# Other shares and other queues for side work: shift sums, helper taps and weight forms in a fused transformer and ConvNeXt kernel

## The chip, the cores and the metric

The kernel runs on one core of a Trainium2 chip. The metric is the device time of one execution in microseconds (us), as the median of several runs. Five engines work in parallel, each on its own instructions in their order: TensorE (PE, matrix products), VectorE (DVE), ScalarE (ACT), GpSimd (POOL) and SyncE (SP). POOL and SP are used here to issue DMAs.

## The reference

For eight images of 384 channels and 32 x 32 pixels, in float32, two layers are computed:

```python
# layer 0, on N = 1024 tokens of C = 384 channels
xn  = layernorm(xf, g1, beta1)
q, k, v = split(einsum('bnc,oc->bno', xn, w_qkv) + b_qkv)        # 8 heads of 48
out = softmax(q @ k.T * 48 ** -0.5) @ v
x1  = einsum('bnc,oc->bno', out, w_proj) + b_proj + xf
h   = gelu(einsum('bnc,oc->bno', layernorm(x1, g2, beta2), w_fc1) + b_fc1)   # 1536 wide
y   = x1 + einsum('bnh,oh->bno', h, w_fc2) + b_fc2
# layer 1, on the image of y
z = depthwise_conv_7x7(y, dw_w) + dw_b
z = gelu((layernorm(z) * ln_w + ln_b) @ w1 + b1)
nx = l2norm_over_pixels(z) / (mean_over_channels(...) + 1e-6)
z = grn_gamma * (z * nx) + grn_beta + z
return y + (z @ w2 + b2)
```

Shifts that the layers add before a product (ln_b, grn_beta, beta1, beta2) are folded into the bias after it: the kernel computes the sums `ln_b @ w1` and `grn_beta @ w2` itself, once, and calls them shift sums here.

## The kernel before

Tokens lie along the free axis and channels on the 128 partitions: an image is a tile of 3 x 1024 columns (`CT` = 3 channel tiles). The images run one after the other. Of image b, PE does the products for q, k and v, then attention (32 steps for each half of the tokens: scores, exponential on ACT, product with v), the projection and the MLP. The second layer's products of image b-1 follow in the same round. The depthwise convolution has no product: DVE does it tap by tap into `acc` (L1102, 42 of 49 taps), during the next image's attention and MLP.

*The helper.* The remaining taps, `HELPED` = 7 of each channel tile and two more in image 0, go another way (`help_convolution`): ACT multiplies half an image by the tap's weight into a tile "res" (L1123), and POOL issues a DMA that adds it to `acc` (L1124). "res" has four buffers. `norm_of_next`, which normalises the next image early, draws its places from the same four (L1717 issues its folds, DMAs that add one half of the partitions to the other). A list `quiet` holds the helper back: while it is not empty, `help_convolution` yields in steps of 1 us, and 3 us more afterwards.

*The order.* All instructions are written out in one order by `Flow`. Each piece of side work is a generator which yields a number of us; `flow.pe(us)` is called behind every piece of PE work and steps the generators that have come due in that planned time. `flow.finish(chain)` writes all that is left of one at once. `end_soon` and `end_convolution` finish the helper and the convolution before the second layer's norm, which the code does in the MLP of each image from 1 on. Each engine then takes its own instructions strictly in this order.

*PSUM.* Pool `ps_s` has two buffers of [128, 1024] (scores, tag "s"), `ps_o` four of [128, 512] (tag "o"). `gelu_half` makes one hidden tile of the MLP in an o buffer, and ACT applies gelu to it (`hid`, L457). In the last image, `mlp_by_halves` does the MLP in two halves of the tokens.

*Image 0.* Beside its attention and MLP the kernel prepares weights: `shift_through_w1` and `shift_through_w2` make the shift sums (DVE scales and adds, a matmul with ones sums the columns into an s buffer, and DVE adds the bias to that, L1501 and L1519, tile `b_f`). `sums_singly` (L1376) and `forms` make sums of weight blocks for a matrix product scheme with fewer multiplications and store them in DRAM (`s_w1`, `s_w2`); `forms` loads its parts as `w_a` and `w_b` and stores them as `s_w`. The MLP's own transfers on POOL are `fc_e<-hid` (L887), `hid<-hid` (L969) and the folds of a norm's sums (`token_sums`, L478), which the matmuls `ln_sum` and `ln_var` (L484) read.

Of the kernel before, what the change touches and what calls it, by code (L numbers as in the profile page):

```python
# [46 lines left out]
F32 = mybir.dt.float32  # L47
AF = mybir.ActivationFunctionType
# [127 lines left out]
def block_kernel(  # L176
# [84 lines left out]
    def o_tile(name):  # L261
        return ps_o.tile([P, NH], F32, tag="o", name=name)

    def weighted(dst, part, name, k):

        if k == 0:
            nc.vector.tensor_scalar(dst, part, col(name, 0), None, ALU.mult)
        else:
            nc.vector.scalar_tensor_tensor(dst, part, col(name, k), dst, ALU.mult, ALU.add)
# [102 lines left out]
            flow.pe(2 * U)  # L372
        return ps

    def linear_half(lhsT, rhs, nk, h, name):
        ps = o_tile(name)
        for k in range(nk):
            nc.tensor.matmul(out=ps, lhsT=lhsT(k), rhs=rhs(k)[:, half(h)], start=(k == 0), stop=(k == nk - 1))  # L378
            flow.pe(U)
        return ps  # L380
# [76 lines left out]
        nc.scalar.activation(dst, src, function, **kw)  # L457
        table[0] = None

    def s_tile(name):  # L460
        return ps_s.tile([P, N], F32, tag="s", name=name)

    def token_sums(t, name, fold, wait, bank):

        width = t.shape[-1]
        if fold is None:
            total = o_tile(name)[:, :width]
            nc.tensor.matmul(out=total, lhsT=ones, rhs=t, start=True, stop=True)  # L470
            flow.pe(U * width / NH)
            return [(total, slice(0, width))]
        rows = [slice(0, 64), slice(64, P)]
        parts = [(fold, slice(0, width))]
        if fold == "columns":
            parts = [(j, slice(j * width // 2, (j + 1) * width // 2)) for j in range(2)]
        for j, cols in parts:
            nc.gpsimd.dma_start(out=t[rows[j], cols], in_=t[rows[1 - j], cols], accum_op=ALU.add)  # L478
        yield wait
        totals = []  # L480
        for j, cols in parts:
            total = bank(f"{name}_{j}")[:, : cols.stop - cols.start]
            for i in rows:
                nc.tensor.matmul(out=total[i, :], lhsT=ones[rows[j], :64], rhs=t[rows[j], cols], start=True, stop=True)  # L484
            flow.pe(U * width / NH / 2)
            totals.append((total, cols))
        return totals

    def layernorm(src, dst, h, eps, g, name, switch, spare=None, spaced=False, slow=1.0, fold=None, wait=3.4, gentle=False, bank=o_tile, late=0):

# [14 lines left out]
            yield 1.2  # L505
        nc.vector.tensor_tensor(a, a, src[:, 2, cols], ALU.add)
        yield 2.6 * slow
        totals = yield from token_sums(a, f"{name}_sum{h}", fold, wait, bank)
        yield 0.8
        for ct in range(CT):  # L510
            for total, part in totals:
# [14 lines left out]
            yield 1.2  # L526
        nc.vector.tensor_tensor(squares[0], squares[0], squares[2], ALU.add)
        yield 1.8 * slow
        totals = yield from token_sums(squares[0], f"{name}_var{h}", fold, wait, bank)
        yield 0.8  # L530

        if not spare:
# [59 lines left out]
    def qk(b, xn, weights=None):  # L592
# [64 lines left out]
        if weights:  # L657
            for _ in fast(0):
                pass
            rest_of_k = fast(1)  # L660
            for n in rest_of_k:
                if n == 9:
                    break
            return parts[:, 0], parts[:, 1], last_tile, ready
# [82 lines left out]
    def attention(b, xt, qT, kT, last_tile, ready, first, next_image):  # L747
# [44 lines left out]
        for n in range(len(steps) + 2):  # L792
            if n == 2:
                last_tile()
            if n < len(steps):
                if steps[n][0] == 0 and steps[n][2] == 0:
                    ready(steps[n][1])
                ps[n] = scores(*steps[n])
            if n >= 2:
                product(*steps[n - 2], ps.pop(n - 2))  # L800
            if n - 2 in (len(steps) // 2 - 9, len(steps) - 9):
                quiet.append("averages")
            if n - 2 == len(steps) // 2 + 6:
                for chain in first:
                    flow.finish(chain)
                xn = one.tile([P, CT, N], F32, tag="xn", bufs=2, name=f"xn2_{b}")
                next_image(b)
                for m in (NP - 1, *range(CT)):
                    flow.finish(chains[0, m])
                proj(b, xt, 0)  # L810
                quiet.clear()
                slow = 1.2 if b in (1, B - 1) else 1.0
                fold = "columns" if b else None
                ln = layernorm(xt, xn, 0, eps0, "g2", f"ln2_{b}", False, spaced=True, slow=slow, fold=fold, wait=4.5)
                ln = flow.spawn(ln)
# [57 lines left out]
                    nc.sync.dma_start(out=other, in_=own)  # L873
                proj("x", xt, qt * P // NH)

    def gelu_half(hid, m, h, xn, weights, wname, name):
        w = weights.at(wname, m // CM)[:, m % CM * CT : (m % CM + 1) * CT, :]
        ps = linear_half(lambda k: w[:, k, :], lambda k: xn[:, k, :], CT, h, f"{name}_{h}_{m}")
        other_table(hid[:, m, half(h)], ps, AF.Gelu, bias=bfc1[:, m : m + 1])

    def difference(dst, more, less):
# [150 lines left out]
    def mlp_by_halves(b, xt, xn, weights, ln, rest, between):  # L1032

        hid = one.tile([P, HT * N], F32, tag="big", name=f"hid_{b}").rearrange("p (m n) -> p m n", m=HT)
        for h in range(2):
            wa, wb = f"fc1_{b}_{h}", f"fc2_{b}_{h}"
            flow.finish(ln)
            for m in range(HT):
                gelu_half(hid, m, h, xn, weights, wa, f"fc1_{b}")
                if m % CM == CM - 1:  # L1040
                    weights.used(wa, m // CM)
                if m == 5 and h == 0:
# [61 lines left out]
            n += 1  # L1104
            yield share * next((early for m, early in first if n <= m), us)

    def help_convolution(acc, us, taken, helped):

        yield 8.0
        for ct in reversed(range(CT)):  # L1110
            taken[ct] = float("inf")
            for i in TAPS[KS * KS - helped :]:
                dy, dx = divmod(i, KS)
                for h in range(2):
                    if quiet:
# [210 lines left out]
    def folds(weights):  # L1326
# [34 lines left out]
                )  # L1361
        nc.vector.tensor_tensor(bout, ps[:, :CT], columns("bproj"), ALU.add)

    def sums_singly(w, store, spare):


# [25 lines left out]
        yield 0.6  # L1392
        plus(r[7], r[14], a22, ALU.subtract)
        plus(r[4], a21, a22)
        yield 0.6
        plus(r[2], a33, r[4], ALU.subtract)
        plus(r[4], r[4], a31)
        yield 0.6
        plus(r[1], a32, r[4])
        minus(r[9], a21, a12)  # L1400
        yield 0.6
        plus(r[9], r[9], a31, ALU.subtract)
        plus(r[0], a31, r[6], ALU.subtract)
        yield 0.6
        nc.vector.tensor_scalar(r[12], a12, -1.0, None, ALU.mult)
        nc.vector.tensor_scalar(r[14], r[14], -1.0, None, ALU.mult)
        yield 1.0
# [2 lines left out]
    def prepare(weights, aside):  # L1410
# [72 lines left out]
        def shift_through_w1():  # L1483
            for i in range(0, HT // 2, CT):
# [12 lines left out]
                for r, a in enumerate((0, 5)):  # L1497
                    for k in range(CT):
                        column_sums(ps, r * CT + k, t[:, k, a, :])
                    m = i + r * HT // 2  # L1500
                    nc.vector.tensor_tensor(b1[:, m : m + CT], ps[:, r * CT : (r + 1) * CT], columns("b1")[:, m : m + CT], ALU.add)  # L1501

        def shift_through_w2():
            for r in range(CT):
# [3 lines left out]
                yield 14.0  # L1508
                h = HT // 2
                for s in range(2):  # L1510
                    g = columns("gbeta")[:, s * h : (s + 1) * h].unsqueeze(2).to_broadcast((P, h, P))
                    nc.vector.tensor_tensor(t[:, s], t[:, s], g, ALU.mult)
                nc.vector.tensor_tensor(t[:, 0], t[:, 0], t[:, 1], ALU.add)
                for k in range(1, h):
                    nc.vector.tensor_tensor(t[:, 0, 0, :], t[:, 0, 0, :], t[:, 0, k, :], ALU.add)
# [3 lines left out]
                nc.vector.tensor_tensor(b2[:, r : r + 1], ps[:, :1], col("b2", r), ALU.add)  # L1519

        if aside:
            yield from shift_through_w1()
# [92 lines left out]
    def main():  # L1615
# [172 lines left out]
        def last_convolution(h, ct, ln=None):  # L1788
# [224 lines left out]
```

## Time and profile before

| | us |
|---|---|
| runs, lowest to highest | 3268.78 to 3273.15 |
| median of three runs | 3271.25 |
| profiled execution, device time | 3271.23 |
| its span in the trace | 3269.3 |
| PE busy | 3231.1 |
| DVE busy | 2423.7 |
| ACT busy | 1670.5 |
| POOL busy | 487.1 |
| mean granted PE clock | 0.995 |

The profile shows one execution. A line of its timeline has the start in us, the time to the end of the group, engine, line of the kernel, operation, written and read tiles, shapes, the number of instructions, and in brackets the idle time before it with what ended that. Its waits list, for a line of an engine, the total of such idle time, how often and the longest. A matmul of 512 float32 columns takes 0.43 us here from start to start where the clock is at 1.00.

### The profile page before, as it was taken

How to read it: one execution, taken by the hardware profiler on the slowest of the kernel's cores; microseconds unless marked ns; L12 is line 12 of the kernel's file. 1: busy time of each engine (PE TensorE's matmuls, PEld its weight loads, DVE VectorE, ACT ScalarE, POOL GpSimd, SP SyncE). 2: the span in 40 equal slices, each digit the busy share in tenths (PEclk: the TensorE clock that was granted, in tenths of full speed). 3: DMA queues.
4: the chain of work that ended last, by engine and by line, in shares of the span. 5: the costliest groups of instructions: out<-in, count | busy, mean ns of one | idle time of the engine just before them, and what ended most of it. 6: DMA issues, size and time to landing. Idle time of an engine off the chain costs nothing. (4 is left out here: it accounts for less than half of the span.)

```text
span 3269.3 us, 38881 instructions
## 1 busy us (share of the span) xinstructions
PE 3231.1 (99%) x14204; PEld 1396.2 (43%) x14204; DVE 2423.7 (74%) x3309; ACT 1670.5 (51%) x2328; POOL 487.1 (15%) x575
## 2 busy tenths in 40 slices
PE   9999998999999999999999999999999999999999
PEld 5334433344344433444344443344434444344455
DVE  4644786678877878678787787876878778879940
ACT  3452664365743566434754537636475365723641
POOL 2111212102211121101212012110121102200000
PEclk9999998999999999999999999999999999999999
DMA  6535744638426473355734465353843638433231
GB/s 214 213 106 121 165 89 75 140 100 193 95 60 161 110 172 80 66 158 125 153 75 98 131 166 125 62 127 105 198 94 58 149 100 196 79 79 91 63 97 54
DMA packets 204114, 387.70 MB, mean 119 GB/s; under 512 B 41232, under 2 KB 46992, under 8 KB 203536
## 3 DMA queue, kind: packets, MB, share of 16 engines
q0 software_dynamic: 82880, 169.38, 27.5%
q1 hardware_dynamic: 120752, 215.09, 21.7%
q8 instruction: 114, 1.87, 0.2%
q10 hardware_dynamic: 288, 0.71, 0.1%
q14 instruction: 80, 0.66, 0.1%
HBM read 199.61 MB, written 38.14 MB: 73 GB/s over the span
## 5 line engine op out<-in xcount | busy, mean ns | idle before, releaser
L1102 DVE SCALAR_TENSOR_TENSOR acc<-pad,vec,acc 128x930 f32<-128x930 f32 (+8 forms) x855 | 956.9, 1156 | 29.2 <-DMA acc<-tap 24.4
L767 ACT ACTIVATE p<-s 128x1024 f32<-128x1024 f32 x512 | 524.3, 1025 | 273.2 <-PE s L758 266.4
L758 PE MATMUL s<-qk 48*64 48x512 f32 x4096 | 539.9, 594 | 5.8 <-DVE b_f L1519 5.6
L778 PE MATMUL o<-p,v 64*64 64x512 f32 x4096 | 536.4, 591 | 0.0
L378 PE MATMUL fc<-xn,fc 128*128 128x512 f32 x1152 | 507.6, 597 | 17.4 <-ACT hid L457 15.3
L1124 POOL DMA_DIRECT2D acc<-tap x306 | 263.4, 874 | 1449.1 <-ACT tap L1123 727.7
L378 PEld LDWEIGHTS fc<-xn,fc 128*128 128x128 f32 x1152 | 218.0, 191 | 302.8 <-issue 271.6
L445 PE MATMUL fc_p<-hid,fc 128*128 128x512 f32 x728 | 318.1, 593 | 2.6 <-DMA hid<-hid 2.0
L778 PEld LDWEIGHTS o<-p,v 64*64 64x64 f32 x4096 | 163.8, 133 | 278.7 <-issue 270.8
L758 PEld LDWEIGHTS s<-qk 48*64 48x64 f32 x4096 | 159.4, 133 | 285.8 <-issue 221.4
L457 ACT ACTIVATE hid<-fc,bfc_f 128x512 f32<-128x512 f32 x192 | 129.4, 684 | 288.1 <-PE fc L378 287.9
L445 PE MATMUL o_p<-y,w 128*128 128x512 f32 x624 | 270.9, 592 | 0.0
L1123 ACT ACTIVATE tap<-pad,vec 128x512 f32<-128x512 f32 x306 | 224.6, 734 | 19.6 <-DMA acc<-tap 19.6
L445 PEld LDWEIGHTS fc_p<-hid,fc 128*128 128x128 f32 x728 | 137.6, 190 | 179.8 <-issue 170.1
L445 PEld LDWEIGHTS o_p<-y,w 128*128 128x128 f32 x624 | 118.0, 190 | 148.7 <-issue 134.9
L1102 DVE SCALAR_TENSOR_TENSOR acc_last<-pad,vec,acc_last 128x377 f32<-128x377 f32 (+24 forms) x288 | 177.2, 690 | 0.6
L891 ACT COPY pad<-x 128x512 f32<-128x512 f32 x48 | 30.2, 635 | 256.2 <-DVE x L957 197.9
L719 DVE TENSOR_TENSOR attn<-o,attn 128x512 f32<-128x512 f32 x64 | 44.1, 690 | 128.9 <-ACT attn L717 128.9
L700 PE MATMUL proj<-attn,wproj_sb 128*128 128x512 f32 x288 | 127.3, 595 | 0.2 <-DVE attn L745 0.2
L678 PE MATMUL v<-wv_sb,xn 128*128 128x384 f32 x384 | 126.8, 487 | 0.0
L432 DVE TENSOR_TENSOR y<-h_n,y 128x512 f32<-128x512 f32 x72 | 49.8, 692 | 62.2 <-PE h_n L416 59.8
L678 PEld LDWEIGHTS v<-wv_sb,xn 128*128 128x128 f32 x384 | 72.5, 190 | 50.1 <-issue 3.3
(376 smaller groups left out, 4052.6 us busy)
## 6 DMA issues: line engine op xcount, KB each, us to landing
acc<-tap POOLq DMA_DIRECT2D x306, 256.0 KB, 3.5
fc<-s_fc SPq DMA_DIRECT2D x91, 256.0 KB, 4.4
w<-s_w SPq DMA_DIRECT2D x72, 320.0 KB, 3.6
hid<-hid POOLq DMA_DIRECT2D x42, 512.0 KB, 7.6
fc<-in_wfc SPq DMA_DIRECT2D x54, 384.0 KB, 4.0
w<-s_w SPq DMA_DIRECT2D x78, 256.0 KB, 2.7
y<-y POOLq DMA_DIRECT2D x36, 512.0 KB, 7.1
w_A<-in_w SPq DMA_DIRECT2D x36, 384.0 KB, 3.2
```

What stands on the lines that cost most here:

```text
L378: nc.tensor.matmul(out=ps, lhsT=lhsT(k), rhs=rhs(k)[:, half(h)], start=(k == 0), stop=(k == nk - 1))
L432: nc.vector.tensor_tensor(c[dst], banks(name), c[other], ALU.add)
L445: nc.tensor.matmul(out=bank, lhsT=lhsT, rhs=rhs, start=k == 0, stop=k == len(pairs) - 1)
L457: nc.scalar.activation(dst, src, function, **kw)
L678: nc.tensor.matmul(out=ps[:, :C], lhsT=xn[:, k, t * P : (t + 1) * P], rhs=wv_sb[:, k, :], start=(k == 0), stop=(k == CT - 1),)
L700: nc.tensor.matmul(out=ps, lhsT=wproj_sb[:, m, ct * P : (ct + 1) * P], rhs=attn[:, m, :], start=(m == 0), stop=(m == CT - 1),)
L758: nc.tensor.matmul(out=s[64 * i : 64 * i + 64, j, :], lhsT=kT[64 * j : 64 * j + HD, m, k0 : k0 + 64], rhs=qT[64 * j : 64 * j + HD, m, half ...
L767: nc.scalar.activation(p, s, AF.Exp)
L778: nc.tensor.matmul(out=outs[i][64 * j : 64 * j + 64, :], lhsT=v[keys, t, at : at + 64], rhs=p[keys, j, :], start=(t == 0), stop=(t == KT - 1),
L1102: nc.vector.scalar_tensor_tensor(dst, window, tap, dst, ALU.mult, ALU.add)
L1123: nc.scalar.mul(t.rearrange("p (h w) -> p h w", w=W), window, tap)
L1124: nc.gpsimd.dma_start(out=acc[:, ct, half(h)], in_=t, accum_op=ALU.add)
```

## The change

Seven edits:

1. Image 0's helper takes 7 taps of each channel tile, as in the others (9 before).
2. The shift sums' biases are added by ACT, a column at a time (15 activations), instead of DVE.
3. `pause()` holds `sums_singly` and `shift_through_w2` back, for up to 24 us at each place, while `quiet` is not empty.
4. `quiet` gets an entry from the second half of the k product until the third step of attention, for images 1 to 7.
5. `next_image`, the load of the next image, is called behind the projection of the first half.
6. Norms draw all their PSUM from the o buffers (the last image's norm used s before), and in image 1 the second layer's norm doesn't fold its squares; in the last image the second half of the hidden tiles uses the two s buffers.
7. The last convolution's first part is paced at 0.72 us a tap (0.66 before).

```diff
-    def linear_half(lhsT, rhs, nk, h, name):
-        ps = o_tile(name)
+    def linear_half(lhsT, rhs, nk, h, name, bank=o_tile):
+        ps = bank(name)[:, :NH]
...
         yield 1.8 * slow
-        totals = yield from token_sums(squares[0], f"{name}_var{h}", fold, wait, bank)
+        if not fold_squares:
+            fold = None
+            yield wait
+        totals = yield from token_sums(squares[0], f"{name}_var{h}", fold, wait)
...
             rest_of_k = fast(1)
+            quiet.append("k")
             for n in rest_of_k:
...
             if n == 2:
                 last_tile()
+                quiet.clear()
...
-                next_image(b)
                 for m in (NP - 1, *range(CT)):
                     flow.finish(chains[0, m])
                 proj(b, xt, 0)
                 quiet.clear()
+                next_image(b)
...
-                gelu_half(hid, m, h, xn, weights, wa, f"fc1_{b}")
+                gelu_half(hid, m, h, xn, weights, wa, f"fc1_{b}", s_tile if h else o_tile)
...
-            for i in TAPS[KS * KS - helped :]:
+            for i in TAPS[KS * KS - HELPED :]:
...
+    def pause():
+        for _ in range(24):
+            if quiet:
+                yield 1.0
...
         nc.gpsimd.dma_start(out=t, in_=w.rearrange("p (g n o) -> p g n o", n=shape[2], o=P))
         yield 9.0
+        yield from pause()
...
-                    m = i + r * HT // 2
-                    nc.vector.tensor_tensor(b1[:, m : m + CT], ps[:, r * CT : (r + 1) * CT], columns("b1")[:, m : m + CT], ALU.add)
+                for r in range(2):
+                    for k in range(CT):
+                        m = i + r * HT // 2 + k
+                        bias = dict(bias=col("b1", m), scale=1.0)
+                        nc.scalar.activation(b1[:, m : m + 1], ps[:, r * CT + k : r * CT + k + 1], AF.Identity, **bias)
...
                 for s in range(2):
+                    yield from pause()
                     g = columns("gbeta")[:, s * h : (s + 1) * h].unsqueeze(2).to_broadcast((P, h, P))
                     nc.vector.tensor_tensor(t[:, s], t[:, s], g, ALU.mult)
+                    yield 1.0
+                yield from pause()
                 nc.vector.tensor_tensor(t[:, 0], t[:, 0], t[:, 1], ALU.add)
                 for k in range(1, h):
+                    yield 0.5
+                    yield from pause()
                     nc.vector.tensor_tensor(t[:, 0, 0, :], t[:, 0, 0, :], t[:, 0, k, :], ALU.add)
-                yield 8.0
+                yield 7.0
                 ps = ps_s.tile([P, N], F32, tag="s", name=f"b2_{r}")
                 column_sums(ps, 0, t[:, 0, 0, :])
-                nc.vector.tensor_tensor(b2[:, r : r + 1], ps[:, :1], col("b2", r), ALU.add)
+                nc.scalar.activation(b2[:, r : r + 1], ps[:, :1], AF.Identity, bias=col("b2", r), scale=1.0)
...
-            helped = HELPED if b else HELPED + 2
-            state["conv"] = flow.spawn(convolution(acc, us, first, taken=taken, helped=helped), paced=True)
-            state["help"] = flow.spawn(help_convolution(acc, 2.7, taken, helped), paced=True)
+            state["conv"] = flow.spawn(convolution(acc, us, first, taken=taken, helped=HELPED), paced=True)
+            state["help"] = flow.spawn(help_convolution(acc, 2.7, taken), paced=True)
...
-                how = dict(wait=5.0, late=3.5) if b < B - 1 else dict(factor=2.4, bank=s_tile)
+                how = dict(wait=5.0, late=3.5, fold_squares=b > 1) if b < B - 1 else dict(factor=2.4)
...
-                conv = convolution(last[0], 0.76 if h else 0.66, (), *rows, ready[h])
+                conv = convolution(last[0], 0.76 if h else 0.72, (), *rows, ready[h])
```

More of the change, by code (lines that the diff above doesn't have):

```diff
@@ L262, in o_tile, with s_tile @@
         return ps_o.tile([P, NH], F32, tag="o", name=name)
+    def s_tile(name):
+        return ps_s.tile([P, N], F32, tag="s", name=name)
     def weighted(dst, part, name, k):
@@ L458, in other_table, with token_sums @@
         table[0] = None
-    def s_tile(name):
-        return ps_s.tile([P, N], F32, tag="s", name=name)
-    def token_sums(t, name, fold, wait, bank):
+    def token_sums(t, name, fold, wait):
         width = t.shape[-1]
@@ L481, in token_sums @@
         for j, cols in parts:
-            total = bank(f"{name}_{j}")[:, : cols.stop - cols.start]
+            total = o_tile(f"{name}_{j}")[:, : cols.stop - cols.start]
             for i in rows:
@@ L487, in token_sums, with layernorm @@
         return totals
-    def layernorm(src, dst, h, eps, g, name, switch, spare=None, spaced=False, slow=1.0, fold=None, wait=3.4, gentle=False, bank=o_tile, late=0):
+    def layernorm(src, dst, h, eps, g, name, switch, spare=None, spaced=False, slow=1.0, fold=None, wait=3.4, gentle=False, late=0, fold_squares=True):
         cols = h if isinstance(h, slice) else half(h)
@@ L507, in layernorm @@
         yield 2.6 * slow
-        totals = yield from token_sums(a, f"{name}_sum{h}", fold, wait, bank)
+        totals = yield from token_sums(a, f"{name}_sum{h}", fold, wait)
         yield 0.8
@@ L874, in exact_attention, with gelu_half @@
                 proj("x", xt, qt * P // NH)
-    def gelu_half(hid, m, h, xn, weights, wname, name):
+    def gelu_half(hid, m, h, xn, weights, wname, name, bank=o_tile):
         w = weights.at(wname, m // CM)[:, m % CM * CT : (m % CM + 1) * CT, :]
-        ps = linear_half(lambda k: w[:, k, :], lambda k: xn[:, k, :], CT, h, f"{name}_{h}_{m}")
+        ps = linear_half(lambda k: w[:, k, :], lambda k: xn[:, k, :], CT, h, f"{name}_{h}_{m}", bank)
         other_table(hid[:, m, half(h)], ps, AF.Gelu, bias=bfc1[:, m : m + 1])
@@ L1105, in convolution, with help_convolution @@
             yield share * next((early for m, early in first if n <= m), us)
-    def help_convolution(acc, us, taken, helped):
+    def help_convolution(acc, us, taken):
         yield 8.0
@@ L1392, in sums_singly @@
         yield 0.6
+        yield from pause()
         plus(r[7], r[14], a22, ALU.subtract)
@@ L1395, in sums_singly @@
         yield 0.6
+        yield from pause()
         plus(r[2], a33, r[4], ALU.subtract)
@@ L1398, in sums_singly @@
         yield 0.6
+        yield from pause()
         plus(r[1], a32, r[4])
@@ L1401, in sums_singly @@
         yield 0.6
+        yield from pause()
         plus(r[9], r[9], a31, ALU.subtract)
@@ L1404, in sums_singly @@
         yield 0.6
+        yield from pause()
         nc.vector.tensor_scalar(r[12], a12, -1.0, None, ALU.mult)
@@ L1510, in shift_through_w2 @@
                 for s in range(2):
+                    yield from pause()
                     g = columns("gbeta")[:, s * h : (s + 1) * h].unsqueeze(2).to_broadcast((P, h, P))
                     nc.vector.tensor_tensor(t[:, s], t[:, s], g, ALU.mult)
+                    yield 1.0
+                yield from pause()
                 nc.vector.tensor_tensor(t[:, 0], t[:, 0], t[:, 1], ALU.add)
                 for k in range(1, h):
+                    yield 0.5
+                    yield from pause()
                     nc.vector.tensor_tensor(t[:, 0, 0, :], t[:, 0, 0, :], t[:, 0, k, :], ALU.add)
-                yield 8.0
+                yield 7.0
                 ps = ps_s.tile([P, N], F32, tag="s", name=f"b2_{r}")
                 column_sums(ps, 0, t[:, 0, 0, :])
-                nc.vector.tensor_tensor(b2[:, r : r + 1], ps[:, :1], col("b2", r), ALU.add)
+                nc.scalar.activation(b2[:, r : r + 1], ps[:, :1], AF.Identity, bias=col("b2", r), scale=1.0)
         if aside:
```

## The prediction

> **What bounds the kernel now.** I read the page's busy times, then every wait of TensorE (PE), then the timeline around the long ones.
>
> ```profile
> PE 3231.1 (99%) x14204; PEld 1396.2 (43%) x14204; DVE 2423.7 (74%) x3309; ACT 1670.5 (51%) x2328; POOL 487.1 (15%) x575
> ```
>
> PE is busy for 99% of the span, the next engine for 74%. So the end is set by PE's stream, and another engine's microsecond counts only where PE stands still. PE's longer waits (total, times, longest):
>
> ```profile
> PE fc L378 <- ACT hid L457: 15.3, 1, 15.3
> PE s L758 <- DVE b_f L1519: 5.6, 1, 5.6
> PE fc L378 <- DVE x L895: 2.2, 1, 2.2
> PE fc_p L445 <- DMA hid<-hid: 2.0, 1, 2.0
> PE h_n L416 <- ACT y L437: 1.8, 1, 1.8
> ```
>
> The first lies in image 1, the second in image 0. A table of 50 us windows shows PE busy for all 50.00 in each from 650 to 2950 us: images 2 to 6 have no wait to lose, and there the change can only add. Line numbers are those of the kernel before. Where a step moves in a queue, I read it from the instruction lists of the two built programs; the durations are the trace's.
>
> **Gain 1, shift sums.** PE's timeline in image 0's attention:
>
> ```profile
> 125.48 1.98 PE L758 MATMUL s<-qk 48*64 48x512 f32 x8 [5.59 <-DVE b_f L1519]
> 127.24 1.93 PE L778 MATMUL o<-p,v 64*64 64x512 f32 x8
> ```
>
> A score waited for a PSUM bank that b_f, an addition of 0.15 us, had still to read; VectorE (DVE) works in order and was full of folding from 112.5 to 125.3. After, ScalarE (ACT) reads the sums: 15 activations of [128,1], which I put at 0.2 us. A softmax step takes 1.02 of ACT's 1.72 us, so 0.7 us a step cover them; without that cover they cost 15 x 0.2 = 3. The wait cost 5.6; then four groups of eight matmuls took 1.71 us instead of 0.86 (half clock; the granted clock of 100 to 150 us is 0.86), 3.4; three small waits on the same banks 1.2 + 0.5. Sum **10.7**.
>
> **Gain 2, the burst in image 1.** ACT's timeline:
>
> ```profile
> 550.98 0.74 ACT L1123 ACTIVATE tap<-pad,vec 128x512 f32<-128x512 f32 x1 [0.86 <-DMA acc<-tap]
> 553.78 0.74 ACT L1123 ACTIVATE tap<-pad,vec 128x512 f32<-128x512 f32 x1 [2.06 <-DMA acc<-tap]
> 554.42 2.40 ACT L457 ACTIVATE hid<-fc,bfc_f 128x512 f32<-128x512 f32 x4
> ```
>
> end_soon finishes the helper, which queues all nine taps left on ACT ahead of the next hid. Two of the four "res" buffers are held by norm_of_next, so each tap waits until the tap two before it has landed (one pair per 4.4 us). PE ran out of banks at 539.9 and stood 15.3. Behind it 60 matmuls took 29.06 instead of 60 x 0.43 = 25.8: 3.3 more. After, image 0 has 42 helped taps instead of 54, and by my list two are left there, ready at about 536.9, 3 us early. But one more DVE tap (1.2) stands before ln_sq, which was done at 524.0 against PE's 524.3: -1.0. Sum 15.3 + 3.3 - 1.0 = **17.6**.
>
> **Gain 3.** Without the two folds of image 1's squares (0.8 us each on GpSimd's queue, POOL, ahead of hid<-hid) I take away the wait of 2.0, less 0.7 for sum matmuls over all 128 rows instead of half of them: **1.3** (0 to 3). In all **29.6**.
>
> **Loss A, image 0's MLP.** pause() stops the w2 sums through the first steps of attention, so forms("w2") comes later: its loads and stores, all issued by 234 us before, now stand in POOL's queue among the MLP's own transfers. That these were met in time:
>
> ```profile
> 268.26 1.19 POOL L887 DMA_DIRECT2D fc_e<-hid  x1 [5.06 <-ACT fc_e L886]
> 269.00 1.31 POOL L478 DMA_DIRECT2D ln_sq<-ln_sq  x1
> 269.55 1.61 POOL L478 DMA_DIRECT2D attn<-attn  x1
> 276.26 0.65 PE L484 MATMUL ln_var<-ln_sq,ones 64*64 64x512 f32 x2
> ```
>
> Six w_a loads (0.54 each, 1.5 MB) now come behind fc_e: the folds issue at about 272.8 and 273.6, with 1.5 MB in front. A fold took 4.8 to 6.2 us to land here: 279 to 280 against PE's 276.3, a stall of **3.5** (0 to 6). Next, the w_b loads wait for eight stores, the last made from DVE's forms: rstd 2.6 us after ln_var, then 15 DVE steps of 0.65, xn and forms, behind which x, hid and the last two forms end near 297; stores and landing (2.4 to 3.3) to 301; seven loads (0.54) to 304.7. Only then hid<-hid issues (294.2 and 296.2 before). At 7.5 us to landing it arrives at 312 to 317; PE's seventh product was at 305.7, with the first stall 309.2. Stall **5.5** (0 to 9). A: **9** (0 to 15).
>
> DMA load speaks for it: 300 to 310 us has a mean busy share of 1.09 before 1.8 MB are added. The Trainium skill, "Trainium Kernel Development and Optimization", Key Constraints, says that queues of SP, ACT and POOL all run on the same 16 DMA engines, so SP's weight loads there compete too; taken whole, that would put A at its upper end.
>
> **Loss B, images 2 to 6.** Five times the same. quiet.append("k") keeps the helper still from the second half of the k product to the third score, some 25 us, and it never catches up: before, one tap stood behind each of hid 4 to 6 and none after; now four (38 and 45, both halves) stand in a row ahead of hid_9. They meet the same two buffers. In image 2 before:
>
> ```profile
> 944.65 1.29 DVE L1730 TENSOR_TENSOR ln<-xn 128x512 f32<-128x512 f32 x2
> 945.85 1.29 DVE L1732 TENSOR_TENSOR ln<-ln,xn 128x512 f32<-128x512 f32 x2
> 946.83 1.67 POOL L1717 DMA_DIRECT2D ln<-ln  x2 [7.39 <-DVE ln L1732]
> 945.28 0.69 ACT L457 ACTIVATE hid<-fc,bfc_f 128x512 f32<-128x512 f32 x1 [0.66 <-PE fc L378]
> ```
>
> Tap 38's transfer stands behind those two folds. On DVE seven taps of the convolution now come before L1732: two fit ahead of ln_sq, four run past rstd (942.6) to 943.3, one more follows xn; L1732 starts at 947.4 to 948.0, take 947.6. In image 1 the same chain ran so: L1732 at 534.2, folds 535.2, tap transfers 536.9, the next tap on ACT at 540.63, its twin at 542.25, that is 6.4 and 8.0 after L1732. Hence hid_9 at 947.6 + 8.0 + 0.65 = 956.3, and PE 0.7 later (554.42 to 555.14 in image 1): 957.0. PE fills four o banks and needs hid_9's again when the fifth tile starts, at 952.85. Stall **4.2** each (3.5 to 5), 5 x 4.2 = **21**; hidden only if the folds are met 4 us earlier.
>
> **The clock.** Half speed followed the idle spells of 5.6 and 15.3 us and cost 3.4 and 3.3; none followed those of 1.8 to 2.2. The seven new stalls of 3.5 to 5.5 lie between: 0 to 7 x 3.3 = 23. Being nearer to 5.6, but shorter, I let two or three pay: **8**.
>
> "TensorE: Matmul & The Clock Gate", Part 1, states that one idle window of about 3.4 us drops the array to half speed, and the windows run freely. By it nearly each of the seven could pay; the sum would be 15 higher. It speaks against this change.
>
> **Loss C, last image, and the rest.** gelu_half's second half takes the two s banks. PE now waits before its third tile for ACT's hid, behind pad, a table load (1.28) and gelu (0.7), instead of 2.2 for x:
>
> ```profile
> 2944.98 7.89 PE L378 MATMUL fc<-xn,fc 128*128 128x512 f32 x18
> 2955.05 5.51 PE L378 MATMUL fc<-xn,fc 128*128 128x512 f32 x12 [2.18 <-DVE x L895]
> ```
>
> DVE, though, gets there sooner: eight of the twelve taps at the end of acc (14.08 us from 2910.06) move into its earlier gaps, so x (2928.70) may come 5 us sooner and the third x (2954.25) near 2949.7; pad 0.7, table 1.3, gelu 0.7 and 0.7 to PE give 953.1, 3 us after PE's 2950.1. So 3.0 for 2.2, less up to 1.3 at the end (h_last): **0** (-2 to +5). next_image's move changes nothing in SP's queue: xn's load keeps its place. The pace of 0.72 and the later ln_7 sums lie beside a full PE: 0, and if that cover failed, DVE is 99% busy from 2950 to 3100 and each tap late costs 0.6.
>
> **Sum.** The profiled execution took 3271.23 (span 3269.3, 1.93 around it), the median of the runs 3271.25. 3271.2 - 29.6 + 9 + 21 + 8 + 0 = **3279.6**.
>
> **Rivals.** (1) *B stays hidden*: tap 38's transfer or its buffer comes free four microseconds earlier than my count, so that ACT reaches hid_9 by 952.1; decided by L1732 before 943.5 or by a third free "res" buffer. For it: PE has 7.7 us of banks. Against: image 1's pairs at 4.4 us. 3271.2 - 29.6 + 9 = 3250.6, or 3242 if A is hidden too; faster. (2) *Stalls without half clock, A partly hidden*: 3271.2 - 29.6 + 21 + 0 to 9 = 3263 to 3272. For it: no drop after 2.2. (3) *Every stall drops the clock*, and A at its end: 3271.2 - 29.6 + 15 + 21 + 23 = 3301. (4) *The change does not do what it says*: column sums still wait for DVE's folding before ACT can read them, and 5.6 + 3.4 remains: 3289. Against: PE's list there now waits for ACT alone.
>
> **How the numbers follow.** Chances: forecast 0.48 (3273 to 3290, mostly slower), (1) 0.2, (2) 0.17, (3) 0.1, (4) 0.05. What a measurement tells from no change is 0.2%, 6.5 us: below 3264.7 lie (1) and a quarter of (2), 0.24; inside to 3277.8 the rest of (2) and the low end of the forecast, 0.22; above, 0.54. Cases of both signs are in play; the forecast's own range is 3273 to 3290. Eight in ten: from (1)'s 3250 to (3)'s 3301.
>
> **What would show it.** Right: the waits on b_f and of 15.3 are gone; PE waits for hid on ACT five times for about 4 us, once in each MLP of images 2 to 6, with taps in pairs on ACT before it, and windows of images 2 to 6 below 50.00; in image 0 ln_var waits for a fold and fc_p for hid<-hid. Wrong: windows of images 2 to 6 still full (then 3242 to 3251), or the wait on b_f under a new reader.

## The result: 0.76% slower

The changed kernel takes 3296.64 us (median of 4 runs, 3293.94 to 3297.94) against 3271.69 (4 runs, 3268.78 to 3273.15): a ratio of 1.0076, 95% interval 1.0059 to 1.0094. Its profiled execution took 3296.53, span 3294.8, so the two profiles lie 25.5 us of span apart. The prediction said slower, 3279.6 with 3250 to 3301 around it. The side was right and the wide range holds the result, near its upper end; the central time is 17 us low, and the narrower range that the forecast gave itself, 3273 to 3290, lies below the result.

The page's busy times after. PE gained 16.6 us of busy time with four instructions fewer: nearly the same work ran slower.

```profile
PE 3247.7 (99%) x14200; PEld 1392.2 (42%) x14200; DVE 2423.2 (74%) x3308; ACT 1668.8 (51%) x2331; POOL 475.4 (14%) x561
```

PE's longer waits after (total, times, longest). Those for b_f and of 15.3 are gone. In their place stand seven waits for hid (five of 3.45 to 3.51, one of 3.15 and a small one), the two of image 0's MLP, and at the end of the last image ln_var:

```profile
PE fc L381 <- ACT hid L460: 20.9, 7, 3.5
PE ln_var L484 <- DMA ln_sq<-ln_sq: 6.0, 1, 6.0
PE fc_p L448 <- DMA hid<-hid: 4.8, 1, 4.8
PE ln_var L470 <- DVE ln_sq L527: 2.8, 2, 2.6
PE h_n L419 <- ACT y L440: 2.2, 1, 2.2
PE h_last L1259 <- DVE acc_last L544: 1.6, 1, 1.6
```

All of PE's listed waits add up to some 42 us, against some 33 before. So 9 us are waiting, and the 16.6 us that are not show in the rows right behind the waits. PE's timeline of the kernel after, three of the new waits:

```profile
268.77 1.12 PE L484 MATMUL ln_var<-ln_sq,ones 64*64 64x512 f32 x2 [5.97 <-DMA ln_sq<-ln_sq]
...
942.84 16.55 PE L381 MATMUL fc<-xn,fc 128*128 128x512 f32 x34 [3.51 <-ACT hid L460]
...
1341.05 17.81 PE L381 MATMUL fc<-xn,fc 128*128 128x512 f32 x34 [3.49 <-ACT hid L460]
```

34 matmuls at full speed take 14.86 (rows of the second experiment, below); here they took 16.55 and 17.81. The windows of 50 us around two of the five waits, which were full before (50.00 busy), show both losses, the idle time and the granted clock (third column from the right):

```profile
900.00:950.00 50.00, 46.49 (x105) 20.15 (x104) 41.96 (x53) 19.99 (x30) 9.32 (x11) 0.97 0.36 64
1300.00:1350.00 50.00, 46.32 (x101) 19.93 (x100) 39.87 (x50) 19.78 (x30) 9.33 (x11) 0.93 0.36 65
```

What made hid late in image 2 is on ACT's timeline of the kernel after: four taps in a row ahead of hid, and ACT idle before the last three until the transfers of earlier taps have landed.

```profile
931.37 0.73 ACT L1128 ACTIVATE tap<-pad,vec 128x512 f32<-128x512 f32 x1
933.11 0.75 ACT L1128 ACTIVATE tap<-pad,vec 128x512 f32<-128x512 f32 x1 [1.01 <-DMA acc<-tap]
939.95 0.74 ACT L1128 ACTIVATE tap<-pad,vec 128x512 f32<-128x512 f32 x1 [6.09 <-DMA acc<-tap]
941.48 0.74 ACT L1128 ACTIVATE tap<-pad,vec 128x512 f32<-128x512 f32 x1 [0.79 <-DMA acc<-tap]
942.12 2.40 ACT L460 ACTIVATE hid<-fc,bfc_f 128x512 f32<-128x512 f32 x4
```

### The profile page after: what moved, and what is told of

It is laid out like the page before. It is cut to its first block, busy times and chain, and to the rows that moved or that the text cites. A ratio compares the mean times of both kernels' runs of the same rounds, so it can differ in the third digit from the quotient of the medians.

```text
span 3294.8 us, 38820 instructions
## 1 busy us (share of the span) xinstructions
PE 3247.7 (99%) x14200; PEld 1392.2 (42%) x14200; DVE 2423.2 (74%) x3308; ACT 1668.8 (51%) x2331; POOL 475.4 (14%) x561
## 4 chain that ended last, share of the span: by engine, by line
PE 81%; DVE 6%; DMA 2%; ACT 1%; issue 1%; SPq 0%; POOL 0%; DVEq 0%; ACTq 0%; POOLq 0%
PE s L762 12%; PE o L782 12%; PE fc_p L448 10%; PE o_p L448 9%; PE fc L381 9%; PE o L1215 4%; PE v L682 3%; PE h_n L419 3%; DVE acc L1107 3%; PE h_z L419 3%; PE h_x L419 3%; PE proj L704 2%; PE h L368 2%; PE qk_n L419 2%; PE h_last L1259 2%; PE qk_z L419 2%
## 5 line engine op out<-in xcount | busy, mean ns | idle before, releaser
L1107 DVE SCALAR_TENSOR_TENSOR acc<-pad,vec,acc 128x930 f32<-128x930 f32 (+7 forms) x861 | 960.6, 1154 | 10.3 <-DMA acc<-tap 6.8
L381 PE MATMUL fc<-xn,fc 128*128 128x512 f32 x1152 | 521.6, 610 | 20.9 <-ACT hid L460 20.9
L1129 POOL DMA_DIRECT2D acc<-tap x294 | 255.4, 888 | 1486.2 <-ACT tap L1128 842.5
L782 PEld LDWEIGHTS o<-p,v 64*64 64x64 f32 x4096 | 157.2, 132 | 282.5 <-issue 277.1
L1128 ACT ACTIVATE tap<-pad,vec 128x512 f32<-128x512 f32 x294 | 214.6, 732 | 43.1 <-DMA acc<-tap 43.1
L1107 DVE SCALAR_TENSOR_TENSOR acc_last<-pad,vec,acc_last 128x551 f32<-128x551 f32 (+22 forms) x288 | 177.1, 686 | 0.5
```

Of the source, the lines that this page charges most:

```text
L782: nc.tensor.matmul(out=outs[i][64 * j : 64 * j + 64, :], lhsT=v[keys, t, at : at + 64], rhs=p[keys, j, :], start=(t == 0), stop=(t == KT - 1),
L1107: nc.vector.scalar_tensor_tensor(dst, window, tap, dst, ALU.mult, ALU.add)
L1128: nc.scalar.mul(t.rearrange("p (h w) -> p h w", w=W), window, tap)
L1129: nc.gpsimd.dma_start(out=acc[:, ct, half(h)], in_=t, accum_op=ALU.add)
```

## The experiments

Each edit is against the kernel named; the kernel before took 3270.6 to 3271.7 in every one of the comparisons. Lines carry the numbers of each kernel's own file.

### Does the waiting of 3.5 us cost more than 3.5 us?

The changed kernel, with four matmuls (3.4 us) put into PE's queue ahead of the tile that waits, in images 2 to 6. Nobody reads their result.

```diff
         for m in range(HT):
+            if m == 1 and isinstance(b, int) and 1 < b < B - 1:
+                busy = s_tile(f"busy_{b}")[:, :NH]
+                for _ in range(4):
+                    nc.tensor.matmul(out=busy, lhsT=ones, rhs=xn[:, 0, half(0)], start=True, stop=True)
             gelu_half(hid, m, 1, xn, weights, wa, f"fc1_{b}")
```

> The changed kernel with four extra matmuls of 128x512 (3.4 us of work that nothing reads) in images 2 to 6, placed right before the hidden tile whose matmuls wait 3.5 us for ScalarE; the order of all other instructions is the same. Theory (the idle spell of 3.5 us drops the clock, and the slow matmuls behind it cost 12.0 us over five images): TensorE is busy where it stood, the wait shrinks to 0.1, the 34 matmuls behind it take 14.6 us again, and the time falls by about 12 to 3284.6 although work was added. Rival (the matmuls behind a stall are slow for another reason, such as late weights or banks): no change, 3295 to 3298.

Measured: 3286.99 us (3285.09 to 3288.11), ratio to the kernel before 1.0051 [1.0034, 1.0068]. The five waits are gone, 17.2 us of matmuls were added, and the program is 9.7 us faster than without them (8.6 when each kernel is taken against the kernel before in its own comparison). If a wait cost only its own length, filling it could at best have changed nothing. The 34 matmuls behind the filled place take 14.86 in all five images, in image 2 for instance:

```profile
941.66 14.86 PE L381 MATMUL fc<-xn,fc 128*128 128x512 f32 x34
```

So the idle spells themselves slowed the work behind them.

The same with one matmul instead of four, which leaves an idle spell of 2.6 us:

> The changed kernel with one extra matmul (0.86 us) instead of four at the same five places: the idle spell shrinks from 3.5 to about 2.6 us, the time at which ScalarE frees the bank stays. Theory (a spell must last some 3 us to cost the clock; those of 1.8 to 2.2 did not): no slow matmuls behind the five waits, 3285 as with four. Rival (the spell's length matters little, the clock drops at any spell that crosses a fixed instant): slow matmuls in part of the five images, 3288 to 3295.

Measured: 3287.2 us (3286.09 to 3288.96), ratio 1.005 [1.0033, 1.0067]. PE's timeline of this kernel, images 2 and 3:

```profile
944.10 14.86 PE L381 MATMUL fc<-xn,fc 128*128 128x512 f32 x34 [2.56 <-ACT hid L460]
...
1340.53 16.55 PE L381 MATMUL fc<-xn,fc 128*128 128x512 f32 x34 [2.62 <-ACT hid L460]
```

Four of the five spells of 2.56 to 2.64 left the 34 matmuls behind them at 14.86, one put them to 16.55. In the changed kernel, spells of 3.45 to 3.51 slowed them in five of five: by 1.7, 3.0, 3.0, 1.4 and 1.7 us, 10.8 in all. In the last image a spell of 3.15 slowed the 30 matmuls behind it in the changed kernel (16.17), and one of 3.2 left them at 13.14 in this run. So a spell's length alone does not decide.

The traces show what does. Within a trace the stretches of half clock start a multiple of 3.413 us apart (in the changed kernel at 633.64, 944.25 and 1340.20, that is 91.0 and 116.0 times 3.413) and last 3.41 us or a multiple of it. Cut into windows on that grid (PE alone), its busy time (the number behind the length) and granted clock (third column from the right) look so for three spells: one of 2.20 in image 1 of the changed kernel, one of 2.18 in the last image of the kernel before, and the one of 3.20 of this run.

```profile
630.23:633.64 3.41, 1.21 (x4) 1.00 0.44 179
633.64:637.05 3.41, 3.41 (x5) 0.50 0.71 282
...
2950.62:2954.03 3.41, 2.25 (x6) 1.00 0.44 115
2954.03:2957.45 3.42, 2.40 (x6) 1.00 0.00 0
2957.45:2960.86 3.41, 3.41 (x10) 1.00 0.45 115
...
2956.03:2959.44 3.41, 2.04 (x5) 1.00 0.14 16
2959.44:2962.85 3.41, 1.58 (x4) 1.00 0.29 99
2962.85:2966.27 3.42, 3.42 (x9) 1.00 0.31 46
```

The spell of 2.20 fell into one window, and the next ran at half clock. The other two were cut by a boundary, into 1.16 and 1.02 and into 1.37 and 1.83, and cost nothing, though one of them is a microsecond longer. Counted over the 14 traces (without their first 75 and last 15 us), a full-clock window in which PE idled for 2.0 us or more was followed by half clock 55 times of 55, one in which it idled for 0.9 to under 2.0 only 5 times of 55. Where a spell falls on the grid is luck: of the spells of 1.8 to 2.3 us 13 of 24 dropped the clock, of those of 2.6 to 3.2 12 of 17 (seven of these 17 are the spell of 2.62 in the change's tail, with one of 1.62 right behind it), of those of 3.4 and more all 33. The price follows from it too: one window at half clock costs up to 1.7 us, two up to 3.4.

### Which part makes the waits?

The changed kernel without the quiet k product:

```diff
             rest_of_k = fast(1)
-            quiet.append("k")
```

> The changed kernel without the one line that puts an entry into quiet at the second half of the k product; all else stays. Theory (that entry makes the helper late, so four taps stand in a row ahead of hid_9 in images 2 to 6): the five waits on hid (3.5 us each, 17.4) and the slow matmuls behind them (12.0) go, 3296.6 - 29.5 = 3267, and some 2 us either way in the last image; windows of images 2 to 6 full again. Rival (the entry only shifts taps, the row of taps comes from finishing the helper before the norm whatever came earlier): 3290 to 3300.

Measured: 3271.91 us (10 runs, 3268.59 to 3276.77), ratio 1.0005 [0.9996, 1.0015]. The five waits for hid are gone, so this one line made them, and it is worth 24.7 us. Images 2 to 6 are full again but for one place. The 24.7 are 3.5 short of the 28.2 that its waits (17.4) and slow matmuls (10.8) cost, and 5 above the time expected: the last image's wait for hid grew from 3.15 to 5.78, and in image 4 a score waits 2.7 for qk, with half clock behind it (0.93 granted from 1550 to 1600 us). The profiled execution took 3276.28, 4.4 above the median, so that wait need not be in every one.

The changed kernel with pause() yielding nothing:

```diff
     def pause():
-        for _ in range(24):
-            if quiet:
-                yield 1.0
+        return
+        yield
```

> The changed kernel with pause() yielding nothing; the shift sums still read by ScalarE. Theory (the late weight forms delay image 0's folds and hid transfers on GpSimd's queue): the waits of 6.0 (ln_var) and 4.8 (hid<-hid) go with the slow matmuls behind them (about 3.4 and 2.8), 3296.6 - 17 = 3280, and the wait on b_f does not come back, since ScalarE reads it. Rival (pause is what took the 5.6 us wait away, ScalarE's reading alone does not): a wait of 4 to 6 us in image 0's attention with its slow matmuls, 3280 + 9 = 3289.

Measured: 3285.9 us (3282.75 to 3286.21), ratio 1.0046 [1.003, 1.0063]. The two waits of image 0's MLP are gone, the wait on b_f does not come back, but the first projection waits 5.95 for attn and then runs at a lower clock: neither the theory nor the rival had this. Without pauses the loads for the next sums are issued in the middle of the attention. DVE's timeline of this kernel, and then of the changed one, at the same step:

```profile
140.60 0.69 DVE L749 TENSOR_TENSOR attn<-attn,r 128x512 f32<-128x512 f32 x1 [11.35 <-DMA r<-back]
```

```profile
134.51 0.69 DVE L749 TENSOR_TENSOR attn<-attn,r 128x512 f32<-128x512 f32 x1 [5.52 <-DMA r<-back]
```

The four r transfers of this step (two of 96 KB, two of 32 KB) were issued between 130.5 and 132.7 in both. Those of 32 KB landed 7.9 us after their issue here (median) and 2.0 us in the changed kernel; from 130 to 135 us the DMA engines are busy for 0.96 here (347 GB/s) and for 0.20 there (61 GB/s). So the pauses pay in the attention and cost in the MLP. (Whether pauses alone, with VectorE still reading the sums, would have taken the wait on b_f away was not run.)

Without either:

> The changed kernel without the quiet entry at k and with pause() yielding nothing. Theory: both savings add, 3296.6 - 29.5 - 17 = 3250, about 21 under the kernel before. Rival (the stalls replace each other, what is saved in one place is waited for in another): 3262 to 3272.

Measured: 3261.47 us (9 runs, 3257.82 to 3263.82), ratio 0.997 [0.996, 0.998]. That is just under the rival's range and 11 above the theory: the projection waits 5.2 and the last image 5.8, both outside the theory. The last image's share was tried by putting its second half back on o banks, on top of that:

```diff
-                gelu_half(hid, m, h, xn, weights, wa, f"fc1_{b}", s_tile if h else o_tile)
+                gelu_half(hid, m, h, xn, weights, wa, f"fc1_{b}")
```

> The changed kernel without the quiet k product and without pauses, and with the last image's second half on o banks again instead of the two s banks. Theory (the last image's wait of 5.8 in the runs without the quiet k product comes from the two s banks): that wait falls to 2.2 as before and with it a clock drop of 3.3 goes, so 3255 to 3258 against 3261.5 with the s banks. Rival (that wait comes from when DVE and ScalarE get to the image, not from the number of banks): it stays above 4 and the time stays at 3260 to 3263.

Measured: 3255.64 us (5 runs, 3253.34 to 3260.26), ratio 0.9955 [0.9942, 0.9969]. The wait disappears altogether (the longest left on acc there is 0.3); before, it was 2.2. The intervals of the two ratios overlap, so that the 5.8 us between the medians rest on the wait's disappearance as much as on the times. With two s banks PE has room for two tiles until ACT has done its chain of pad, table load and gelu; with four o banks that chain is covered.

### What are the gains worth one by one?

The kernel before with ScalarE reading the shift sums (the two edits of b1 and b2 in the diff above), nothing else:

> The kernel before with the shift sums' biases added by ScalarE, nothing else. Theory (transfers of image 0 come due as PE does: with the wait on b_f gone, the loads r<-back meet the weight loads and proj waits some 5 to 6 us for them, as without pause): the wait of 5.6 and its 3.4 of slow matmuls go, 1.7 of small waits too, 5.5 and 2 come back, 3270.6 - 10.7 + 7.5 = 3267. Rival (the shift sums were the only late thing there): 3270.6 - 10.7 = 3260.

Measured: 3272.77 us (10 runs, 3270.25 to 3277.39), ratio 1.0007 [0.9997, 1.0016]: nothing gained, and above both forecasts. PE's wait on b_f is gone, and a wait of 3.7 for attn at the first projection, two of 1.0 for w_gbeta and one of 1.2 for qk have taken its place. PE only came sooner to the next late thing.

The kernel before with seven helped taps in image 0:

```diff
-            helped = HELPED if b else HELPED + 2
+            helped = HELPED
```

> The kernel before with seven helped taps in image 0 instead of nine, nothing else. Theory (the 15.3 us wait is those taps queued ahead of hid): the wait and the 3.3 us of slow matmuls go, 3270.6 - 18.6 = 3252, with up to 2 us less if the convolution, now two taps per tile longer, makes a norm late. Rival (42 taps still meet the end of the helper, half of the wait stays): 3260 to 3266.

Measured: 3255.14 us (3253.89 to 3257.18), ratio 0.9953 [0.9936, 0.9969], 15.5 below the kernel before and close to the theory. The wait of 15.3 is gone, and that for hid<-hid is down to 0.5 with the folds still in place. With image 1's squares not folded as well (the `fold_squares` lines of the diff above):

> The kernel before with seven helped taps in image 0 and no fold of image 1's squares; everything else of the change left out. Theory (gain 3 alone is worth 1.3 or less, because the wait for hid<-hid is 0.5 once the seventh tap is in): 3254 to 3255, the same as seven taps alone. Rival (the forecast's gain 3 stands by itself): 3253 or less.

Measured: 3252.82 us (5 runs, 3249.91 to 3256.61), ratio 0.9945 [0.9932, 0.9959]. That is the rival's time, but the 2.3 between it and seven taps alone lie well inside both intervals, so a gain of the missing folds is not shown. It is the fastest median of the study and beats both kernels. With ScalarE's shift sums on top of these two:

> The kernel before with three of the edits: shift sums on ScalarE, seven taps, no fold of image 1's squares. Against the run without the quiet entry and pause (3261.5) only the last image differs, which is as in the kernel before. Theory (two s buffers for the hidden tiles make the last image's wait 5.8 instead of 2.2, and the norm's o buffers and the slower pace bring the wait of 2.6 on ln_sq): 3261.5 - 3.6 - 1.7 - 2.6 = 3253.5. Rival (the tail's waits are set by DVE anyway, the banks do not matter): 3260 to 3263.

Measured: 3258.88 us (5 runs, 3252.94 to 3262.03), ratio 0.9956 [0.9942, 0.997]. That lies between the two forecasts. Again ScalarE's sums give nothing: the wait on b_f (4.7 with the sums on DVE) is exchanged for 4.0 at the projection and for 1.3 and 0.9 on w_gbeta and w_lnb. (The wait of 2.2 at a score in this trace lies at 1559 us, in image 4, like that of 2.7 above.) In this run the last image's tail is that of the kernel before, and the wait of ln_var there (2.6 in every run with the change's tail) is gone.

### Is the projection's wait due to the loads?

To that kernel, with ScalarE's sums, seven taps and no fold, the pauses of the routine that adds up w1t, and no others:

> The kernel before with the shift sums read by ScalarE, seven helped taps in image 0, no fold of image 1's squares, and the pauses in the routine that loads and adds the w1 and qk weights alone: in image 0's attention the two large loads stay off the queues until the projection, while nothing is paused in the MLP (the w2 sums run as before) and image 0's k product is not made quiet. Theory (the projection's wait of 4.0 in the runs without pauses is the 32 KB transfers that stand among those loads): the wait on attn goes, ln_var and fc_p of image 0's MLP wait as little as before (at most 2), and the median is 3250 to 3254, 4 to 8 less than the same kernel without the pauses. Rival (the wait comes from DVE's order, not from transfers): the wait on attn stays at about 4 and the median stays at 3257 to 3260. Second rival (the loads, held back, meet the MLP's own transfers): the wait moves to ln_var or hid<-hid and the time is 3260 or more.

Measured: 3258.55 us (5 runs, 3253.88 to 3265.45), ratio 0.9959 [0.9946, 0.9973]. The edit did not do what it was meant for: the same loads were issued at 125 to 135 us, since by the program's order they stand in POOL's queue before `quiet` is set, and the projection waited 3.8 in the profiled execution, the slowest of the five. It tells nothing of the two theories. So the loads were held themselves, with a list of its own that is set 16 softmax steps before the end of the first query half and cleared behind the projection, and the next image's load was put behind it too:

```diff
+    def held():
+        for _ in range(60):
+            if hold:
+                yield 1.0
...
+        yield from held()
         nc.gpsimd.dma_start(out=t, in_=w.rearrange("p (g n o) -> p g n o", n=shape[2], o=P))
...
+                yield from held()
                 t = blocks(f"w2_gbeta_{r}")
```

> The kernel before with the shift sums read by ScalarE, seven helped taps in image 0, no fold of image 1's squares, the next image's load behind the projection, and no pause but one: the loads of the w1t and w2 parts that would be issued in the last 16 softmax steps of image 0's first query half are held until its projection is emitted. By the built program one w1t load and the second w2 pair move behind the projection; the MLP's own transfers meet only the last four stores of the w2 forms. Theory (the wait of 4.0 at the projection comes from the small r transfers that share the DMA engines with those loads): the wait on attn falls below 1.5 and no clock drop follows it, the median is 3246 to 3252, 5 to 12 less than the same kernel with the loads in place (3258.9). Rival (that wait comes from the order on VectorE, not from transfers): the wait on attn stays at about 4, the median at 3257 to 3260. Second rival (a later load makes something else late): the wait on attn goes, ln_var or fc_p of image 0's MLP waits 3 or more instead, and the time is 3256 or more.

Measured: 3254.19 us (6 runs, 3250.36 to 3258.4), ratio 0.995 [0.9938, 0.9961]. The first projection no longer waits (PE is busy for 49.92 of 100 to 150 us and for 50.00 of 150 to 200). But the loads came later, and the wait came with them, at the second projection. Rows of this kernel's timeline, of SP, POOL, DVE and PE; first the step that leads to the first projection, then the one to the second:

```profile
135.99 0.58 SPq L727 DMA_DIRECT2D sums<-attn  x1
137.95 0.20 DVE L730 RECIPROCAL inv<-sums 128x8 f32<-128x8 f32 x1 [1.99 <-DMA sums<-attn]
...
200.85 0.58 SPq L727 DMA_DIRECT2D sums<-attn  x1
201.05 3.19 POOL L1442 DMA_DIRECT2D w_a<-in_w  x6
206.66 0.20 DVE L730 RECIPROCAL inv<-sums 128x8 f32<-128x8 f32 x1 [5.24 <-DMA sums<-attn]
214.79 9.10 PE L704 MATMUL proj<-attn,wproj_sb 128*128 128x512 f32 x14 [5.12 <-DVE attn L749]
```

The same transfer of 4 KB landed 1.4 us after its issue had ended at 136.57, with the DMA engines busy for 0.07 (135 to 140 us), and 5.2 us after 201.43, when six loads of w_a had been issued beside it and they were busy for 0.68 and 0.87 (200 to 205 and 205 to 210 us). That is the theory's mechanism, at another place, and nearly the second rival's outcome: the wait follows the loads. (Two loads were moved at the first projection, POOL's and the next image's, so their shares there are not told apart; at the second it is POOL's alone.)

## Why the prediction was right, and where its sum was off

**The side and the cause** were right: the quiet k product makes PE wait for hid once in each of images 2 to 6. The chain of B held closely: seven taps stand before the second addition of the folds, which starts at 933.63 in image 2, and hid follows at 942.12, 8.5 later against the 8.65 counted. That the helper "never catches up" and that ACT's taps go in a row is in ACT's rows above; that the one line does it is shown by its removal. The rival that B stays hidden is refuted. (Of the windows called full in the kernel before one, 1650 to 1700 us, shows 49.93; nothing rests on it.)

**The clock was mis-sized**, and this is the step that failed. The text put it at 8 of 0 to 23, because the spells lay between 2.2 (no drop) and 5.6 (drop). Every one of the seven dropped it, and so did the last image's: 10.8 us in images 2 to 6, 3.2 and 2.6 behind the waits of ln_var and fc_p (granted clock 0.68 and 0.74 over the 10 us behind them), 3.0 in the last image, where no drop had been counted: 19.6. The inference from length was unsafe below 2.2 as well: that the kernel before lost nothing behind its spells of 1.8 to 2.2 was luck, and the same wait for y in image 1, 2.20 long in the changed kernel, did drop the clock. So did the tail's spells of 2.62 and 1.62. Image 1 and the tail lost 1.7 us each so (0.83 granted from 632 to 642 and from 3174 to 3184 us), where the prediction had nothing. The rival "every stall drops the clock", which was given a chance of 0.1, is what happened to the clock, and its 3301 is nearest to the measured time, though its 15 for A was not needed. The Trainium skill's page "TensorE: Matmul & The Clock Gate", Part 1, had put the threshold at one idle window of about 3.4 us: the five spells of 3.45 to 3.51 agree with it. The drops after 2.20, 2.62 and 3.15 do not, if a whole window must be idle: 2.0 us of a window were enough here, and there the measurement decides.

**The other terms.** Of the sum's error of 15.0, 14.0 is clock, gains included; the others nearly cancel.

| term | predicted | measured, from the two profiles |
|---|---|---|
| gains 1 to 3 | -29.6 | -32.3 (waits 5.6, 1.7, 15.3 and 2.0; clock 2.9, 1.7 and 3.1) |
| A, image 0's MLP, waits | +9 | +10.8 (6.0 and 4.8) |
| B, five waits | +21 | +17.4 (3.5 each, against 4.2) |
| clock behind new waits | +8 | +19.6 |
| clock behind the spells of image 1 and the tail | 0 | +3.4 |
| C, last image and tail, waits | 0 | +4.5 (3.15 for 2.2; ln_var 2.6; small ones) |
| sum | +8.4 | +23.4, of 25.5 in the spans |

The 2.1 left over was not traced. In gain 1 the price behind b_f was 2.9 and not 3.4: of the four groups three took 1.7 and one 1.15; a second half-clock stretch, at 141.5 us, cost 1.7 that the prediction did not list, and it went too. ScalarE's activations took 0.27 each, not 0.2, and cost nothing that shows. In A the folds were issued at 259.4 and 261.8, behind the six w_a loads as reckoned, but the first met PE only at 268.8, after some 9 us instead of the 4.8 to 6.2 taken from the kernel before. A landing time from rows with no loads in front did not hold behind 1.5 MB; the Trainium skill's "Trainium Kernel Development and Optimization", Key Constraints, had said that the queues of SP, ACT and POOL share the same 16 DMA engines, and the run with the loads held agrees: a transfer of SP took 1.4 us without and 5.2 us beside POOL's loads. In C the count of the middle of the image was right (3.0 for 2.2 reckoned, 3.15 found), but it was not given the clock's price, and the tail's ln_var was missed.

**Gains** came nearly as counted in the changed kernel, but gain 1 is not a gain of its edit: ScalarE reading the sums alone gives nothing, twice. It was had because the pauses also kept the loads off the r transfers. The prediction saw what the pauses cost in the MLP, and not what they pay in the attention. It also had wrong when they act: image 0's q and k products make no entry in `quiet`, so nothing is held in the first steps of its attention; there `quiet` holds from fifteen steps before the first projection until behind it, and again before the second (VectorE's folding of w_gbeta stops after 122.0 us and goes on at 152.95). Gain 2 stands by itself: 15.5 in the run with seven taps alone.

## To carry to other kernels

A spell that PE waits through costs its length and, in all cases from 3.4 us on and in about half of them at 2 us, 1.4 to 3.4 us more of half clock. So cost five small waits with the clock on them, and look first whether a few tiles more of independent matmuls, or one buffer more, cut each below 2 us. Before a wait is taken away, ask what PE meets next and how late that is: here a wait of 5.6 turned into one of 4 a few steps on. Small transfers on the critical path (4 to 32 KB) should have no large loads issued beside them; here the loads were on POOL's queue and the transfers on SP's.

## What the runs showed of the hardware

- 17.2 us of useless matmuls made the program 9.7 us faster, since they kept the clock up over idle spells of 3.5 us.
- Idle spells and the clock: half clock began on a grid of 3.413 us, 55 times of 55 behind a window with 2.0 us or more of idle PE, 5 times of 55 behind one with 0.9 to under 2.0. By length, 13 of 24 spells of 1.8 to 2.3 us dropped it, 12 of 17 of 2.6 to 3.2, 33 of 33 of 3.4 and more. The price of a drop varied between 1.4 and 3.4 us for spells of like length, with one or two windows at half clock.
- A transfer of 4 KB took 1.4 us to land with the DMA engines at 0.07 and 5.2 us at 0.68 to 0.87; the r transfers of 32 KB took 2.0 us at 0.20 and 7.9 us at 0.96 (medians).
